# A graph layer on one core: shorter row scans, norms behind the first keys, queries mixed two chunks ahead

## The chip, the core and the metric

The kernel runs on one core of a Trainium2 chip. The core has a matrix engine (PE, with its weight loads PEld), a vector engine (DVE), an activation engine (ACT), a general engine (POOL[...]) and SyncE (SP), which here only issues DMAs. ACT and POOL issue DMAs too. The metric is the device time of one execution in microseconds, as the median of several.

## What is computed

One layer of a graph network with linear attention and a mixture of experts, all in float32, for 10,000 nodes with 512 features and 160,000 edges sorted by destination (more edges go to low node numbers: the destination is 10000 u², u uniform).

```
xn  = layernorm(x)
gnn = relu(segment_sum((xn @ W)[src] * edge_weight, dst) + bias)
q, k, v = split(xn @ w_qkv.T)            # 8 heads of 64
ctx = softmax(k over nodes).T @ v        # 64 x 64 per head
mix = layernorm((softmax(q) * 64**-0.5 @ ctx) @ w_out.T) * gamma
x1  = x + gnn + mix
out = x1 + sum_e weight_e * (gelu(layernorm(x1) @ W1_e + b1_e) @ W2_e + b2_e)
```

The six expert weights come from a router that sees the mean of the normalised rows of x1.

## The kernel before

**Chunks and tiles.** The nodes are cut into 20 chunks of 512 rows (the last has 272), a row of a chunk being partition p, sub-row s of 4. The edges are cut into 1250 tiles of 128. Edges are summed by windows: two tiles per window for the first 448 windows (`PAIRED`), one tile after that, so 802 windows; four windows make a group, 201 groups in all.

**Start.** Rows of x are loaded, normalised (DVE for the statistics, ACT and POOL for the rows) and stored to `xn_d` (`normal_rows`, L357). `norms` (L516) squares the 512 x 512 weights wk and then wq on ACT, sums the columns on PE and takes the maximum on DVE; `as_they_are` (L525) turns both into a factor 0 or 1, `usable`, spread to all partitions by a small product (L531). Every exponential of keys and queries is scaled by it (L765, L772). The two squares share one buffer, so the second can't be written before PE has read the first.

**Keys stage** (L744 to L793). For each chunk PE makes the keys (`pk`, 4 x 4 products of 128 x 512), the queries (`pq`, as many), the transposed rows of the next chunk, the context products `pc` (16), and the transposed queries, which ACT's queue stores to `qT_d`. From chunk 3 on, `place_edges` (L394) has prepared the edges: each edge's place in its window, `bases` (the first node of each window) and `jump` (the rows that a window skips). `count` collects checks whose total must be `ALL_GOOD`; otherwise a slow general path runs behind the branch at L615. `find_rows` (L444) finds for each node the row of its sum: for each of the 4 sub-rows one pass over all 802 windows compares `bases` with the node's number, multiplies by `jump` and sums up. It does five chunks as the edges are placed and then one per chunk.

**Edges.** For each tile POOL gathers 128 rows of `xn_d` (L485, 256 KB), DVE makes a selection matrix, and PE multiplies it with the rows (`pm`, L503). ACT copies a group's sums out and its queue stores them to `part_d`. There are 24 buffers for gathered rows. PE's order is the order of the program, written out by hand: after each product `work(us)` (L597) adds up the time of the products so far, and `edges_to` puts in as many groups as that time divided by `PACE` (0.93 us) allows. Nodes whose edges lie in several windows are put together by `carry` (L560), which reads stored sums back, adds and stores again.

**Mixing and node sums** (L872 to L965). `attention(c)` loads the transposed queries (`qT`, one buffer, SP's queue) and the rows of x (`xt`), multiplies the queries with the mixed context (`po`, 16 products), takes layer statistics and adds x; the result is `ot`. In its last quarter it calls `nodes_rows`, in which PE transposes the gathered node sums of the chunk in turn (`at` to `aT`) and POOL gathers the next chunk's by `row_of` (L865). Then `pg` multiplies `aT` with the graph weights (16 products), DVE adds bias, relu and `ot`, and SP stores x1 to `x1_d`. In this version attention runs one chunk ahead of the node sums: `po` 0, then for each c `po` c+1 and `pg` c. `far_enough` (L846) makes sure that the edges that a gather needs are summed; for chunk 18 all of them, with the last carry.

**Experts.** From L1233 on PE multiplies chunk after chunk, full to the end.

Of the kernel before, what the change touches and what calls it, by code (L numbers as in the profile page):

```python
# [9 lines left out]
F32 = mybir.dt.float32  # L10
I32 = mybir.dt.int32
AF = mybir.ActivationFunctionType
ALU = mybir.AluOpType
# [3 lines left out]

P = 128
SQ = 32
SUB = 4  # L20
EPS = 1e-5
HEAD = 64
QSCALE = HEAD ** -0.5
PAIRED = 448
GROUP = 4
WIN = P // GROUP
# [1 line left out]
EARLY = 3  # L28
ROWS_SOON = 5
PRODUCT = 0.83  # L30
PACE = 0.93

AT_HAND = [(5, 320), (7, 384), (9, 448), (11, 512), (13, 576), (14, 640), (15, 672), (16, 704), (17, 736), (18, 756)]
CARRIES = [0, 128, 224, 320, 384, 448, 512, 576, 640, 672, 704, 736, 756]
# [12 lines left out]
def gps_layer_kernel(  # L47
# [19 lines left out]
    nc = tc.nc  # L67
    N, D = x.shape
    NET = src.shape[1]
    KB = D // P  # L70
# [9 lines left out]
    chunks = []  # L80
# [6 lines left out]
    NCH = len(chunks)  # L87
# [64 lines left out]
    def behind(inst, other):  # L152

        tc.add_manual_dep(inst.ins, other.ins.name, mybir.DependencyInfo(
            mybir.DependencyClass.NoSync, mybir.DependencyReason.SCHED_ONLY), reason="order of work")
# [179 lines left out]
    with ExitStack() as ph:  # L335
# [50 lines left out]
        on_w = ep.tile([P, NET], F32, name="on_w")  # L386
        bases = ep.tile([P, NW + 1], F32, name="bases")
        jump = ep.tile([P, NW], F32, name="jump")
        count = ep.tile([P, 2 + len(AT_HAND)], F32, name="count")
        n_big = ep.tile([1, 2], F32, name="n_big")  # L390
        usable = ep.tile([P, 1], F32, name="usable")
        n_odd = ep.tile([1, 1], I32, name="n_odd")
# [1 line left out]
        def place_edges():  # L394
            nc.sync.dma_start(src_sb, src)
            nc.sync.dma_start(w_sb, edge_w)
            dst_sb = tmp.tile([P, NET], I32, name="dst_sb", tag="whole")
            nc.sync.dma_start(dst_sb, dst)
            row_sb = tmp.tile([P, NET], I32, name="row_sb")
            nc.sync.dma_start(row_sb, dst[0:1, :].to_broadcast([P, NET]))  # L400

            nc.vector.memset(bases[:, 0:1], 0.0)
            nc.vector.memset(bases[:, NW:], FAR)
            nc.vector.tensor_copy(bases[:, 1:PAIRED],
                                  row_sb[:, 2 : 2 * PAIRED].rearrange("p (w j) -> p w j", j=2)[:, :, 0])
            nc.vector.tensor_copy(bases[:, PAIRED:NW], row_sb[:, 2 * PAIRED :])
            gap = ew.tile([P, NW], F32, name="gap", tag="past", bufs=1)
            nc.vector.tensor_tensor(gap, bases[:, 1:], bases[:, :NW], ALU.subtract)
            nc.vector.tensor_copy(place, dst_sb)

            def by_window_of(t, per_window, o, op):

                nc.vector.tensor_tensor(
                    o[:, : 2 * PAIRED].rearrange("p (w j) -> p w j", j=2),
                    t[:, : 2 * PAIRED].rearrange("p (w j) -> p w j", j=2),
                    per_window[:, :PAIRED, None].to_broadcast([P, PAIRED, 2]), op)
                nc.vector.tensor_tensor(o[:, 2 * PAIRED :], t[:, 2 * PAIRED :], per_window[:, PAIRED:NW], op)

            by_window_of(place, bases, place, ALU.subtract)

            by_window_of(place, gap, on_w, ALU.is_equal)
            nc.vector.tensor_tensor(on_w, on_w, w_sb, ALU.mult)


            nc.vector.memset(jump[:, 0:1], 1.0)
            nc.vector.tensor_scalar(jump[:, 1:], gap[:, : NW - 1], -1.0, float(WIN), op0=ALU.mult, op1=ALU.add)


            good = tmp.tile([P, NET], F32, name="good", tag="whole")
            by_window_of(place, gap, good, ALU.is_le)  # L430
            nc.vector.scalar_tensor_tensor(good, place, 0.0, good, op0=ALU.is_ge, op1=ALU.mult)
            nc.vector.scalar_tensor_tensor(good, place, float(WIN - 1), good, op0=ALU.is_lt, op1=ALU.mult,
                                           accum_out=count[:, 0:1])
            nc.vector.tensor_scalar(good[:, :NW], gap, 0.0, None, op0=ALU.is_ge)
            nc.vector.scalar_tensor_tensor(good[:, : NW - 1], gap[:, : NW - 1], float(WIN), good[:, : NW - 1],
                                           op0=ALU.is_lt, op1=ALU.mult, accum_out=count[:, 1:2])

            for i, (n, w) in enumerate(AT_HAND):
                nc.vector.tensor_scalar(count[:, 2 + i : 3 + i], bases[:, w : w + 1],
                                        float(chunks[n][0] if n < NCH else N), None, op0=ALU.is_ge)  # L440

        ALL_GOOD = P * (NET + NW - 1 + len(AT_HAND))

        def find_rows(c, other):  # L444

            at = ew.tile([P, SUB], F32, name="at")
            for s in range(SUB):
                past = ew.tile([P, NW], F32, name="past", bufs=1)
                scan = nc.vector.scalar_tensor_tensor(
                    past, bases[:, :NW], node[:, c, s : s + 1], jump,  # L450
                    op0=ALU.is_le, op1=ALU.mult, accum_out=at[:, s : s + 1])
                if other:
                    behind(scan, other)
            nc.vector.tensor_tensor(at, at, node[:, c], ALU.add)
            nc.vector.tensor_scalar(row_of[:, c], at, float(ZERO_ROW), None, op0=ALU.min)

# [58 lines left out]

        def norms(i, w):  # L516

            sq = b_io.tile([P, KB, D], F32, name="sq", tag="ek")
            nc.scalar.activation(sq, w, AF.Square)
            pn = psum.tile([1, D], F32, name="pn", tag="ps")  # L520
            for kb in range(KB):
                nc.tensor.matmul(pn, ones, sq[:, kb, :], start=kb == 0, stop=kb == KB - 1)
            nc.vector.tensor_reduce(n_big[:, i : i + 1], pn, axis=AX.X, op=ALU.max)

        def as_they_are():  # L525


            nc.vector.tensor_scalar(n_big, n_big, NORM2, None, op0=ALU.is_le)
            nc.vector.tensor_tensor(n_big[:, 0:1], n_big[:, 0:1], n_big[:, 1:2], ALU.mult)
            pn = psum.tile([P, 1], F32, name="pn", tag="ps")  # L530
            nc.tensor.matmul(pn, until[0:1, :], n_big[:, 0:1], start=True, stop=True)  # L531
            nc.vector.tensor_copy(usable, pn)

# [202 lines left out]
            transposed(xnT, xn, chunks[c][1], psum, "ps")  # L736
            return xnT

        norms(0, wk)
        norms(1, wq)  # L740
        as_they_are()
        xn = rows_of(0)
        xnT = turned_rows(0, xn)
        for c, (_, r) in enumerate(chunks):  # L744
# [13 lines left out]
            if c + 1 < NCH:  # L758
                xn_next = rows_of(c + 1)
            ek = b_io.tile([P, SUB, D], F32, name="ek")  # L760
            for s in range(SUB):
                pk = psum.tile([P, D], F32, name="pk", tag="ps")
                times(pk, xnT, s, r, wk)
                work(KB * PRODUCT)
                nc.scalar.activation(ek[:r, s, :], pk[:r], AF.Exp, scale=usable[:r])  # L765
                nc.vector.tensor_tensor(kacc[:r], kacc[:r], ek[:r, s, :], ALU.add)
            qt = b_io.tile([P, SUB, D], F32, name="qt")
            for s in range(SUB):
                pq = psum.tile([P, D], F32, name="pq", tag="ps")
# [105 lines left out]
            return qT  # L875

        def rows_again(c):
            xt = io.tile([P, SUB, D], F32, name="xt")
            nc.sync.dma_start(xt[: chunks[c][1]], tokens(x, c))
            return xt  # L880

# [6 lines left out]
        def attention(c, beside):  # L888


            r = chunks[c][1]
            qT = queries_in(c)
            xt = rows_again(c)
            ot = io.tile([P, SUB, D], F32, name="ot", bufs=3)
            for s in range(SUB):
                if s == SUB - 1:
                    beside()
                po = psum.tile([P, D], F32, name="po", tag="ps")
                times(po, qT, s, r, mix)
                put_out(KB * PRODUCT)  # L900
                if c == s == 0:
                    held["at"] = gathered(0)
                nc.scalar.copy(ot[:r, s, :], po[:r, :])  # L903
            mv = small.tile([P, SUB, 2], F32, name="mv")
            row_stats(ot, r, mv)
            for s in range(SUB):
                nc.vector.scalar_tensor_tensor(ot[:r, s, :], ot[:r, s, :], mv[:r, s, 0:1],
                                               gamma_b[:r], op0=ALU.subtract, op1=ALU.mult)
                nc.vector.scalar_tensor_tensor(ot[:r, s, :], ot[:r, s, :], mv[:r, s, 1:2],
                                               xt[:r, s, :], op0=ALU.mult, op1=ALU.add)  # L910
            return ot

        ot_next = attention(0, lambda: None)
        for c, (_, r) in enumerate(chunks):
            ot, at = ot_next, held["at"]
            aT = io.tile([P, KB, SUB * P], F32, name="aT", bufs=1)

            def nodes_rows():
# [1 line left out]
                if c + 1 < NCH:  # L920
                    held["at"] = gathered(c + 1)

            if c + 1 < NCH:
                ot_next = attention(c + 1, nodes_rows)
            else:
                nodes_rows()

# [393 lines left out]
```

## Time and profile before

| What | Value |
|---|---|
| median of 3 runs | 3378.7 us (3378.27 to 3379.26) |
| profiled execution | 3381.44 us |
| its span in the trace | 3379.6 us |
| granted PE clock, mean | 0.988 of full |
| PE busy | 3270.7 us, 97% |
| DVE, ACT, POOL busy | 55%, 24%, 42% |
| keys begin on PE | 43.0 us |
| gathers of edges begin, end on POOL | 169.9, 1904.3 us |
| keys stage ends on PE | 1138.9 us |
| experts begin on PE | 2009.6 us |

In the lines that follow a timeline row gives start and duration in microseconds, engine, line, operation, output and input, the number of instructions, and in brackets the idle time of the engine just ahead and what ended it. A row of groups gives busy time and the mean of one in nanoseconds, then the idle time. A row of waits gives total, number and longest. In the slices each digit is the busy share of one fortieth of the span in tenths. Records of PE are half products: each float32 product has two.

### The profile page before, as it was taken

The page shows a single profiled execution, that of the slowest core. Times are in us where ns is not written, and L with a number is a line of the kernel's source. Part 1 is how long each engine was busy: PE and PEld are TensorE (multiplying, and loading weights), DVE is VectorE, ACT ScalarE, POOL GpSimd, SP SyncE. Part 2 cuts the span into 40 slices and gives each one's busy share as a digit, 9 for nine tenths or more (in the row PEclk, how much of TensorE's full clock was granted, in tenths as well). Part 3 has the DMA queues.
Part 4 walks back from the last instruction along what each step waited for, and adds up shares of the span by engine and source line. Part 5 has one row for each costly group of instructions (what it writes and reads, how often), then busy time and mean ns, then how long its engine had stood idle before and what let it go on. Part 6 is the DMA issues. An engine that isn't in the chain of part 4 may idle for free.

```text
span 3379.6 us, 37367 instructions
## 1 busy us (share of the span) xinstructions
PE 3270.7 (97%) x12969; PEld 1923.8 (57%) x12969; DVE 1842.5 (55%) x4771; ACT 797.3 (24%) x1626; POOL 1433.4 (42%) x1472
## 2 busy tenths in 40 slices
PE   6999999999999899999999999999999999999998
PEld 3444444444443333333333347888888888888886
DVE  7844545455545456666766576544554455445543
ACT  4412121212121121122222123222222222222211
POOL 6667777777777777777777420000000000000000
PEclk9999999999999999999999999999999999999999
DMA  9778888888878888999989751121212121212111
GB/s 363 262 231 254 275 258 279 257 272 263 268 241 262 290 291 304 309 329 325 329 313 329 235 163 50 50 63 50 88 50 63 54 84 50 63 60 78 50 39 40
DMA packets 218332, 644.96 MB, mean 191 GB/s; under 512 B 35486, under 2 KB 75422, under 8 KB 193786
## 3 DMA queue, kind: packets, MB, share of 16 engines
q0 software_dynamic: 108208, 354.02, 33.5%
q1 hardware_dynamic: 67656, 168.51, 15.2%
q10 hardware_dynamic: 42266, 119.91, 9.1%
q8 instruction: 106, 1.74, 0.2%
q14 instruction: 96, 0.79, 0.1%
HBM read 485.32 MB, written 157.00 MB: 190 GB/s over the span
## 4 chain that ended last, share of the span: by engine, by line
PE 54%; DMA 9%; issue 1%; DVE 1%; POOL 1%; ACT 0%; POOLq 0%; DVEq 0%; ACTq 0%; SPq 0%
PE px L1103 15%; PE pz L1103 10%; PE py L1103 10%; PE po L205 7%; DMA msg<-xn_d,src_sb 6%; PE pg L205 6%; PE pm L503 3%; PE ph L1103 2%; PE pt L197 1%; DMA z_d<-xt 1%; POOL msg L485 1%; DMA xt<-x_d 1%; DMA at<-part_d,row_of 1%; DMA x_d<-ot 0%; PE pcarry L568 0%
## 5 line engine op out<-in xcount | busy, mean ns | idle before, releaser
L485 POOL DMA_INDIRECT msg<-xn_d,src_sb x1250 | 1226.5, 981 | 424.8 <-issue 236.6
L503 PE MATMUL pm<-msg,sel 128*32 128x512 f32 x2504 | 356.2, 603 | 28.7 <-DMA msg<-xn_d,src_sb 28.6
L492 DVE TENSOR_SCALAR sel<-iota_w,place,w_sb 128x31 f32<-128x31 f32 x1250 | 305.9, 317 | 103.9 <-PE pm L503 103.7
L205 PE MATMUL po<-G,qT 128*128 128x512 f32 (+1 forms) x640 | 292.7, 604 | 8.0 <-DMA qT<-qT_d 8.0
L205 PE MATMUL pg<-wq,aT 128*128 128x512 f32 (+1 forms) x640 | 293.5, 607 | 5.9 <-ACT aT L199 5.9
L779 PE MATMUL pc<-xn,ek 128*128 128x512 f32 (+1 forms) x640 | 288.7, 601 | 3.7 <-DVE qt L190 3.7
L205 PE MATMUL pk<-wk,xnT 128*128 128x512 f32 (+1 forms) x640 | 285.7, 599 | 0.0
L205 PE MATMUL pq<-wq,xnT 128*128 128x512 f32 (+1 forms) x640 | 284.5, 597 | 0.0
L506 ACT COPY part<-pm 128x512 f32<-128x512 f32 x201 | 118.1, 587 | 629.7 <-PE pm L503 604.7
L503 PEld LDWEIGHTS pm<-msg,sel 128*32 128x32 f32 x2504 | 68.3, 109 | 282.2 <-issue 196.9
L205 PEld LDWEIGHTS pg<-wq,aT 128*128 128x128 f32 (+1 forms) x640 | 116.9, 189 | 182.9 <-issue 162.9
L205 PEld LDWEIGHTS po<-G,qT 128*128 128x128 f32 (+1 forms) x640 | 116.0, 189 | 171.0 <-issue 147.5
L205 PEld LDWEIGHTS pk<-wk,xnT 128*128 128x128 f32 (+1 forms) x640 | 118.1, 188 | 164.4 <-issue 153.1
L205 PEld LDWEIGHTS pq<-wq,xnT 128*128 128x128 f32 (+1 forms) x640 | 117.5, 187 | 165.3 <-issue 159.2
L1103 PE MATMUL px<-xnT,w_sb 128*128 128x256 f32 (+1 forms) x800 | 203.8, 377 | 6.4 <-DVE u L1138 6.3
L779 PEld LDWEIGHTS pc<-xn,ek 128*128 128x128 f32 (+1 forms) x640 | 118.7, 192 | 145.8 <-issue 141.7
L1103 PE MATMUL px<-w_sb,hh 128*128 128x256 f32 (+1 forms) x800 | 185.7, 379 | 0.0
L161 DVE BATCH_NORM_STATS2 st<-ot 128x6 f32<-128x512 f32 (+1 forms) x160 | 110.2, 689 | 138.4 <-ACT ot L903 137.5
L1103 PE MATMUL py<-xs,w_sum 128*128 128x256 f32 (+1 forms) x800 | 185.0, 374 | 0.0
L1103 PE MATMUL py<-w_sum,hh 128*128 128x256 f32 (+1 forms) x800 | 179.2, 379 | 0.0
L1103 PEld LDWEIGHTS px<-xnT,w_sb 128*128 128x128 f32 x800 | 150.3, 191 | 28.5 <-DVE u L1138 8.8
L1103 PEld LDWEIGHTS py<-w_sum,hh 128*128 128x128 f32 (+1 forms) x800 | 150.0, 188 | 22.7
(270 smaller groups left out, 4438.5 us busy)
## 6 DMA issues: line engine op xcount, KB each, us to landing
part_d<-part ACTq DMA_DIRECT2D x201, 256.0 KB
msg<-xn_d,src_sb POOLq DMA_INDIRECT x1250
xn<-in_x SPq DMA_DIRECT2D x19, 1024.0 KB
xn_d<-xn ACTq DMA_DIRECT2D x19, 1024.0 KB
qT_d<-qT ACTq DMA_DIRECT2D x19, 1024.0 KB
qT<-qT_d SPq DMA_DIRECT2D x19, 1024.0 KB
xt<-in_x SPq DMA_DIRECT2D x19, 1024.0 KB
x_d<-ot SPq DMA_DIRECT2D x19, 1024.0 KB
```

Source lines behind the costliest of these rows:

```text
L161: nc.vector.bn_stats(st[:r, s, :], t[:r, s, :])
L197: nc.tensor.transpose(pt[:, s * r : (s + 1) * r], t[:r, s, kb * P : (kb + 1) * P], ident[:r, :r])
L205: nc.tensor.matmul(po[:r, :], t[:, kb, s * r : (s + 1) * r], w[:, kb, :], start=kb == 0, stop=kb == KB - 1)
L485: nc.gpsimd.indirect_dma_start(out=m[k], out_offset=None, in_=xn_d, in_offset=bass.IndirectOffsetOnAxis(ap=src_sb[:, t0 + k : t0 + k + 1], ...
L492: nc.vector.tensor_scalar(sel[:, k, 1:], iota_w, place[:, t0 + k : t0 + k + 1], w_sb[:, t0 + k : t0 + k + 1], op0=ALU.is_equal, op1=ALU.mult)
L503: nc.tensor.matmul(pm[h * WIN : (h + 1) * WIN, :], sel[:, k, :], m[k] if k < len(m) else m[0], start=j == 0, stop=j == batch - 1, skip_gro ...
L506: nc.scalar.copy(part, pm)
L779: nc.tensor.matmul(pc, ek[:r, s, cb * P : (cb + 1) * P], xn[:r, s, :], start=s == 0, stop=s == SUB - 1)
L1103: nc.tensor.matmul(o, lhs[j], rhs[j], start=start and j == 0, stop=stop and j == n - 1, skip_group_check=True)
```

## The change

It has these parts:

- `find_rows` passes only over the windows that can hold the chunk's nodes: a range worked out from the expected distribution, ten tiles wider on both sides (`SPARE`), with one more instruction that adds what lies ahead of the range. Forty checks (`spans_hold`) join `count`. The scan's output no longer shares a buffer with `gap`.
- The norms of wk and wq, and the factor `usable`, are made after the four key products of chunk 0 instead of ahead of the transposes; the four exponentials and sums of chunk 0 follow them. The squares use the buffer `qT` instead of `ek`, and their sums the two banks of the edges.
- Attention runs two chunks ahead: `po` 0, `po` 1, then for each c `po` c+2 and `pg` c. `ot` has four buffers instead of three, `xt` one instead of two.
- `PACE` is 0.945 instead of 0.93.

```diff
-PACE = 0.93
+PACE = 0.945
...
         def find_rows(c, other):
             at = ew.tile([P, SUB], F32, name="at")
+            lo, hi = span(c)
             for s in range(SUB):
-                past = ew.tile([P, NW], F32, name="past", bufs=1)
+                past = ew.tile([P, WIDEST], F32, name="past_c", bufs=1)[:, : hi - lo - 1]
                 scan = nc.vector.scalar_tensor_tensor(
-                    past, bases[:, :NW], node[:, c, s : s + 1], jump,
+                    past, bases[:, lo + 1 : hi], node[:, c, s : s + 1], jump[:, lo + 1 : hi],
                     op0=ALU.is_le, op1=ALU.mult, accum_out=at[:, s : s + 1])
...
+            nc.vector.tensor_scalar(at, at, bases[:, lo : lo + 1], float(1 + lo * WIN), op0=ALU.subtract, op1=ALU.add)
...
+        def window_at(node, more):
+            tile_no = NET * (node / N) ** 0.5 + more
+            return min(max(int(tile_no / 2 if tile_no < 2 * PAIRED else tile_no - PAIRED), 0), NW)
+
+        def span(c):
+            return window_at(chunks[c][0], -SPARE), window_at(chunks[c][0] + SUB * chunks[c][1], SPARE)
+
+        def spans_hold():
+            for c, (b, r) in enumerate(chunks):
+                for i, w, op, edge in ((0, span(c)[0], ALU.is_le, b), (1, span(c)[1], ALU.is_ge, b + SUB * r)):
+                    at = 2 + len(AT_HAND) + 2 * c + i
+                    nc.vector.tensor_scalar(count[:, at : at + 1], bases[:, w : w + 1], float(edge), None, op0=op)
...
         def norms(i, w):
-            sq = b_io.tile([P, KB, D], F32, name="sq", tag="ek")
+            sq = b_io.tile([P, KB, D], F32, name="sq", tag="qT")
...
-            pn = psum.tile([1, D], F32, name="pn", tag="ps")
+            pn = psum_e.tile([1, D], F32, name="pn", tag="pm")
...
-        norms(0, wk)
-        norms(1, wq)
-        as_they_are()
...
+            sums = []
             for s in range(SUB):
                 pk = psum.tile([P, D], F32, name="pk", tag="ps")
                 times(pk, xnT, s, r, wk)
                 work(KB * PRODUCT)
-                nc.scalar.activation(ek[:r, s, :], pk[:r], AF.Exp, scale=usable[:r])
-                nc.vector.tensor_tensor(kacc[:r], kacc[:r], ek[:r, s, :], ALU.add)
+                sums.append(pk)
+                if c == 0 and s < SUB - 1:
+                    continue
+                if c == 0:
+                    norms(0, wk)
+                    norms(1, wq)
+                    as_they_are()
+                for i, pk in enumerate(sums):
+                    at = s + 1 - len(sums) + i
+                    nc.scalar.activation(ek[:r, at, :], pk[:r], AF.Exp, scale=usable[:r])
+                    nc.vector.tensor_tensor(kacc[:r], kacc[:r], ek[:r, at, :], ALU.add)
+                sums = []
...
-            xt = io.tile([P, SUB, D], F32, name="xt")
+            xt = io.tile([P, SUB, D], F32, name="xt", bufs=1)
...
-            ot = io.tile([P, SUB, D], F32, name="ot", bufs=3)
+            ot = io.tile([P, SUB, D], F32, name="ot", bufs=4)
...
-        ot_next = attention(0, lambda: None)
+        mixed = [attention(c, lambda: None) for c in range(2)]
         for c, (_, r) in enumerate(chunks):
-            ot, at = ot_next, held["at"]
+            ot, at = mixed.pop(0), held["at"]
...
-            if c + 1 < NCH:
-                ot_next = attention(c + 1, nodes_rows)
+            if c + 2 < NCH:
+                mixed.append(attention(c + 2, nodes_rows))
             else:
                 nodes_rows()
```

More of the change, by code (lines that the diff above doesn't have):

```diff
@@ L19 @@
 SQ = 32
+SPARE = 10
 SUB = 4
@@ L388, in gps_layer_kernel @@
         jump = ep.tile([P, NW], F32, name="jump")
-        count = ep.tile([P, 2 + len(AT_HAND)], F32, name="count")
+        count = ep.tile([P, 2 + len(AT_HAND) + 2 * NCH], F32, name="count")
         n_big = ep.tile([1, 2], F32, name="n_big")
@@ L406, in place_edges @@
             nc.vector.tensor_copy(bases[:, PAIRED:NW], row_sb[:, 2 * PAIRED :])
-            gap = ew.tile([P, NW], F32, name="gap", tag="past", bufs=1)
+            gap = ew.tile([P, NW], F32, name="gap", bufs=1)
             nc.vector.tensor_tensor(gap, bases[:, 1:], bases[:, :NW], ALU.subtract)
@@ L440, in place_edges @@
                                         float(chunks[n][0] if n < NCH else N), None, op0=ALU.is_ge)
-        ALL_GOOD = P * (NET + NW - 1 + len(AT_HAND))
+            spans_hold()
+        ALL_GOOD = P * (NET + NW - 1 + len(AT_HAND) + 2 * NCH)
+        WIDEST = 256
+        def window_at(node, more):
[8 more added lines that the diff above has]
+                    nc.vector.tensor_scalar(count[:, at : at + 1], bases[:, w : w + 1], float(edge), None, op0=op)
         def find_rows(c, other):
             at = ew.tile([P, SUB], F32, name="at")
+            lo, hi = span(c)
             for s in range(SUB):
-                past = ew.tile([P, NW], F32, name="past", bufs=1)
+                past = ew.tile([P, WIDEST], F32, name="past_c", bufs=1)[:, : hi - lo - 1]
                 scan = nc.vector.scalar_tensor_tensor(
-                    past, bases[:, :NW], node[:, c, s : s + 1], jump,
+                    past, bases[:, lo + 1 : hi], node[:, c, s : s + 1], jump[:, lo + 1 : hi],
                     op0=ALU.is_le, op1=ALU.mult, accum_out=at[:, s : s + 1])
@@ L529, in as_they_are @@
             nc.vector.tensor_tensor(n_big[:, 0:1], n_big[:, 0:1], n_big[:, 1:2], ALU.mult)
-            pn = psum.tile([P, 1], F32, name="pn", tag="ps")
+            pn = psum_e.tile([P, 1], F32, name="pn", tag="pm")
             nc.tensor.matmul(pn, until[0:1, :], n_big[:, 0:1], start=True, stop=True)
```

## The prediction

> **What bounds the kernel now.** I read the page's slices first, then the timelines of PE and POOL, then PE's waits. In the slices PE is full nearly everywhere, and POOL is steady until slice 23 and then silent:
>
> ```profile
> PE   6999999999999899999999999999999999999998
> POOL 6667777777777777777777420000000000000000
> ...
> L485 POOL DMA_INDIRECT msg<-xn_d,src_sb x1250 | 1226.5, 981 | 424.8 <-issue 236.6
> L503 PE MATMUL pm<-msg,sel 128*32 128x512 f32 x2504 | 356.2, 603 | 28.7 <-DMA msg<-xn_d,src_sb 28.6
> ```
>
> A gather takes POOL 0.98 us and 0.30 us to issue, so POOL's 0.75 share is a full engine. By its timeline the gathers run from 169.9 to 1904.3. In the keys stage (to 1138) PE is the slower: POOL's gaps over 0.7 us there end at "PE pm", 27 us in all. From 1138 on POOL hardly stops: 517 edge and 72 node gathers in 766.3 us, **1.30 us each**. There PE waits on landings. Its work in 1138.95 to 1917.3, warm and without waits, is some 688 us: 138 products of `po` and `pg` by 3.55 (490), edge sums 135, transposes 34, carries 18, context 12. That leaves 90 us of 778 for waits and cold clock. From 2009.6 PE is full to the end (the experts). So three stretches matter: the start, POOL's chain, and what PE has left after the last edge.
>
> ```profile
> 20.18 5.97 PE L522 MATMUL pn<-sq,ones 128*1 128x512 f32 x8 [20.18 <-ACT sq L519]
> 28.15 5.29 PE L522 MATMUL pn<-sq,ones 128*1 128x512 f32 x8 [2.00 <-ACT sq L519]
> 39.07 0.55 PE L531 MATMUL pn<-n_big,until 1*128 1x1 f32 x2 [5.63 <-DVE n_big L529]
> 39.55 3.68 PE L197 MATMUL pt<-ident,xn 128*128 128x128 f32 x16
> 43.02 15.12 PE L205 MATMUL pk<-wk,xnT 128*128 128x512 f32 x32
> ```
>
> This is PE's timeline at the start (start, duration): keys begin at 43.0, behind both norms, though wk was there at 18.1 (the Square that reads it) and chunk 0's rows were normalised at 15.9.
>
> ```profile
> PE pm L503 <- DMA msg<-xn_d,src_sb: 28.6, 21, 5.0
> ...
> PE po L205 <- DMA qT<-qT_d: 8.0, 1, 8.0
> PE pt L197 <- DVEq L615: 7.2, 1, 7.2
> ...
> PE pc L779 <- DVE qt L190: 3.7, 2, 3.2
> ```
>
> PE's waits (total, times, longest) are few; the longest in the middle are landings of messages, one load of qT, and the branch at L615.
>
> ```profile
> 413.75 1.05 DVE L449 SCALAR_TENSOR_TENSOR past<-bases,node,jump 128x802 f32<-128x802 f32 x1
> 413.88 1.74 POOL L485 DMA_INDIRECT msg<-xn_d,src_sb  x1 [0.30 <-DMA msg<-xn_d,src_sb]
> ...
> 1903.34 1.02 POOL L485 DMA_INDIRECT msg<-xn_d,src_sb  x1 [0.31 <-issue]
> 1944.66 0.95 POOL L865 DMA_INDIRECT at<-part_d,row_of  x1 [40.30 <-DMA b_sb<-in_b]
> ```
>
> ```profile
> 1915.45 1.93 PE L503 MATMUL pm<-msg,sel 128*32 128x512 f32 x6 [0.99 <-DMA msg<-xn_d,src_sb]
> 1917.31 8.15 PE L205 MATMUL pg<-wq,aT 128*128 128x512 f32 x16
> ...
> 2009.59 1.03 PE L1103 MATMUL px<-xs,w_sum 128*128 128x256 f32 x4
> ```
>
> Both engines at the end of the edges: the last gather is issued at 1904.3, its sum is done at 1917.3, and 92.3 us of PE's work still stand before the experts at 2009.6.
>
> **Norms behind the first keys.** Keys need the last odd row of chunk 0 (15.9) and then the 3.5 us that lay between the first transpose and `pk` before: 19.4. Keys 15.1 (as before, cold): 34.5. Norm of wk 3.5 (8 records by the warm 0.43): 38.0. The square of wq shares one buffer (now tag qT) with that of wk, so it can't start earlier: 1.9 of ACT plus a handover, PE idle 2.0: 40.0. Norm of wq 4.4: 44.4. Then DVE's chain to `n_big`, 1.0 of work, 5.6 before because other work was queued ahead; I take 3.3: 47.7. With the small product (0.55) and half a cold restart (0.9) the queries begin at 49.1 instead of 57.98: **-8.9**, between -4.7 (full 5.6, both restarts cold) and -13 (1.0, none). Queued behind the wait on PE are only the queries; behind it on ACT the four exponentials, which hold four of six banks, so two query products can go first.
>
> [...] after waits of 1.86 and 3.21 us the 16 records of `pc` at 123.85 took 8.80 instead of 7.03, and after 2.39, 0.48 and 0.48 us again 8.83. I take half of a 1.8 us loss, hence 4.4[...].
>
> **Short scans.** The 802-element scan holds DVE 0.98 us. Ranges worked out from L449's edges are 27 to 145 windows wide, mean 53; the nearest row, the same operation 128 wide (L565), takes 0.33, so 0.25 to 0.3 each, -0.72. Of DVE's packed stretch from 88 to 160, 20 scans save 14.4; 40 new checks cost 0.07 each (three of L439 take 0.26) = 2.8, the new subtraction 5 x 0.08: net -11.2. PE's waits there (1.86, 3.21, 2.39, 0.48, 0.48) and two cold restarts of 1.8 are 12 us, but PE also comes 8.9 earlier to a DVE that is only 8.4 earlier at the first `pc` and 11.3 at the second. So the edges stage begins **9 us** earlier (3 to 13), which is start and scans together. The last chunk's scans (3 us sooner at the branch) lie inside POOL's chain and give nothing; without that cover they'd give 3.
>
> [...] a gather beside a scan took 1.74 instead of 0.95, two per chunk, 15 chunks, 24 us of POOL. By the row I take POOL as full as its 24 buffers allow at the end of the keys[...].
>
> **PACE 0.945.** By the rules of L584 to L604 the keys end after 88 groups of 8 tiles instead of 90, and 6.7 tiles into the next (17 chunks x 48 products x 0.83, less 6 x 0.945, is 671.6; by 0.945, 710.7 tiles). PE saves 16 sums by 0.232 = 3.7. POOL, limited by buffers, is then 22 ahead: 726 gathers issued instead of 733, so 596 follow instead of 589: 7 x 1.30 = +9.1. Net **+5.4** on POOL's end, with the 9 earlier: 1900.7; last sum, by the same 13.0 of landing and work, 1913.7.
>
> **Queries two chunks ahead.** Ahead of the last edge now stand po 19's first quarter and all of pg 16: 7 products of 3.5 more. A second wait for qT (one buffer, 8.0, then `po` 6.33 instead of 3.60) appears as po 2 follows po 1 with no pg between; its DMA stands on SP as before. With 3.7 of sums PE has about 744 us of work against POOL's 788, so these are hidden in POOL's chain; without it they'd cost 10.7 plus nothing moved. xt's single buffer is asked for one chunk period (some 40 us) after its last reader, against a load of 8: nothing. POOL's gathers of node rows keep their places among the edges (at 17 behind tile 1248). SP's store of x1 and the load of qT are no further apart than now.
>
> After the last sum PE has: two products po 19 (7.0), transposes 1.9, wait for the last carry, carry 2.0, po 3.5, pg 17 13.8, transposes 1.8, pg 18 13.8, statistics and transposes 2.0, the wait for ACT 5.9 as now, pg 19 16.0. The carry needs the last part written and read: 1917.3 to 1923.5 for the write, some 4 for the reads, so 10.5 against PE's 8.8: wait 1.7. Sum 69.3 instead of 92.3: **-23.0**. Gather 18 lands about 14.6 after the carry and PE wants it after 17.3; gather 19 stands behind the weights' issues, as before, and lands under ACT's 5.9. If that cover is gone, 3 to 6 us. DVE has some 49 us of work in these 69.
>
> **Sum.** -9.0 + 5.4 - 23.0 = -26.6. Bounds of what I can't see (DVE crowded in the shorter tail, POOL stopping on full buffers when PE's two qT waits fall together) are 0 to +10; I take 5: -21.6 on the span of 3379.6, 3358.0. The profiled execution took 3381.4, 1.8 around the span, and stands 2.7 over the median 3378.7; from the median, **3357 us**, 3350 to 3365 alone.
>
> **Rivals.** (1) The start is swallowed and the tail half used: rows and DVE keep chunk 3 where it was (-3), DVE sets the tail (-12), PACE +5.4: -9.6, 3369. For it: DVE is 46 of 50 us busy in 50 to 100. (2) Everything: 13 at the start, no tail loss, -30.6, 3348. (3) Nothing: POOL's chain ends later by what the tail gives, 3379; needs POOL 20 us late, against its full rate. (4) Slower: PE becomes the bound in the mixing stage, if qT of each chunk comes late behind other waits on SP. Price: 18 chunks by the 8 us of a bare qT load, less the 44 us that PE has to spare, 100; it decides from 2.4 us per chunk on. Against it: qT is issued 19.5 us ahead of use now (1226.6 for 1246.1) and lands in 8. Taken at 2.9 us per chunk it gives 3388.
>
> **How the numbers follow.** A change of 0.2% (6.8 us) is about what a measurement tells from none. Forecast 0.55, (1) 0.20, of which a third ends within 0.2%, (2) 0.15, (3) 0.04, (4) 0.06: faster 0.83, same 0.11, slower 0.06. Leaving out 2 in 10 (some of (2)'s best end, part of (1) and (3), and (4)) gives 3344 to 3371.
>
> **What would show it.** Keys at 19 to 21 us; queries near 49; edge sums from about 198; the last gather near 1900; a second wait of `po` on qT near 1200; after the last sum about 70 us to the experts. It is wrong if the last gather comes after 1910, if PE waits on DVE in the tail, or if `pm` no longer waits for messages at all.

## The result, and the profile after

| | before | after |
|---|---|---|
| median | 3378.98 us (4 runs, 3378.27 to 3384.84) | 3362.78 us (4 runs, 3361.17 to 3366.16) |
| ratio after / before | | 0.995, 95% interval 0.9932 to 0.9967 |
| profiled execution | 3381.44 us | 3361.17 us |
| its span | 3379.6 us | 3359.4 us |
| chunk 3's keys begin | 193.15 | 182.82 |
| keys stage ends | 1138.9 | 1124.7 |
| last gather of edges ends | 1904.3 | 1903.5 |
| last edge sum ends on PE | 1917.3 | 1914.9 |
| experts begin on PE | 2009.6 | 1984.7 |
| experts, begin to end of span | 1370.0 | 1374.7 |

The kernel is 16.2 us faster by the medians and 20.2 by the two profiled spans. The runs fell into two conditions of the chip, a first one in which the kernel before takes 3375 to 3379 us, and a second one in which it takes 3648 to 3651 us and PE, DVE and ACT pause while edges are gathered (151 us on PE in the changed kernel); the table above, the kernel before profiled again and the run with half of the gathers are of the first, the other experiments of the second, and times are compared within a condition only.

First the slices and groups of the kernel after.

```profile
PE   7999999999999879999999989999999999999998
...
POOL 6677777777777677777777520000000000000000
...
L505 POOL DMA_INDIRECT msg<-xn_d,src_sb x1250 | 1214.0, 971 | 434.5 <-issue 238.8 <-PE pm L523 70.4 <-DMA msg<-xn_d,src_sb 59.2
L523 PE MATMUL pm<-msg,sel 128*32 128x512 f32 x2504 | 345.8, 602 | 12.2 <-DMA msg<-xn_d,src_sb 11.9
```

The shape is as before: PE full, POOL steady and then silent. PE waits 11.9 us for messages where it waited 28.6, and POOL waits 70.4 us for PE to free buffers where it waited 54.0.

PE's timeline at the start shows keys at 18.62 and queries at 51.09, behind a wait of 7.78 us.

```profile
18.62 15.07 PE L206 MATMUL pk<-wk,xnT 128*128 128x512 f32 x32
33.62 3.59 PE L542 MATMUL pn<-sq,ones 128*1 128x512 f32 x8
39.21 3.59 PE L542 MATMUL pn<-sq,ones 128*1 128x512 f32 x8 [2.00 <-ACT sq L539]
50.58 0.58 PE L551 MATMUL pn<-n_big,until 1*128 1x1 f32 x2 [7.78 <-DVE n_big L549]
51.09 15.97 PE L206 MATMUL pq<-wq,xnT 128*128 128x512 f32 x32
```

PE's waits (total, times, longest) show the second load of `qT`, and one that no line of before had in this size, `px` for DVE's `u`.

```profile
PE po L206 <- DMA qT<-qT_d: 16.9, 2, 8.6
...
PE pm L523 <- DMA msg<-xn_d,src_sb: 11.9, 16, 2.5
PE px L1131 <- DVE u L1166: 10.9, 4, 6.7
PE pn L551 <- DVE n_big L549: 7.8, 1, 7.8
PE pt L198 <- DVEq L635: 6.7, 1, 6.7
```

PE's timeline from the last edge sum into the experts:

```profile
1913.31 1.67 PE L523 MATMUL pm<-msg,sel 128*32 128x512 f32 x8 [0.21 <-DMA msg<-xn_d,src_sb]
1914.90 7.08 PE L206 MATMUL po<-G,qT 128*68 128x512 f32 x16
...
1965.78 0.98 PE L198 MATMUL pt<-ident,at 68*128 68x68 f32 x3 [4.35 <-DMA at<-part_d,row_of]
...
1984.67 1.03 PE L1131 MATMUL px<-xs,w_sum 128*128 128x256 f32 x4
...
1996.75 2.07 PE L1131 MATMUL px<-xnT,w_sb 128*128 128x256 f32 x4 [6.73 <-DVE u L1166]
```

The tail from the last sum to the experts is 69.8 us instead of 92.3. Twelve microseconds into the experts PE stands for 6.73 us. ACT's timeline says why: its copy to `u` waits for the store of the last chunk's x1, because `u` now lies in memory that held that chunk's `ot`.

```profile
1995.87 0.37 ACT L1165 COPY u<-px 128x256 f32<-128x256 f32 x1 [8.13 <-DMA x_d<-ot]
```

In the kernel before ACT waited 7.49 us for the same store, but at the first gelu, where PE needed nothing of it.

### The profile page after: what moved, and what is told of

Read it like the earlier page. It is cut to its first block, busy times and chain, and to the rows that moved or that the text cites. A ratio compares the mean times of both kernels' runs of the same rounds, so it can differ in the third digit from the quotient of the medians.

```text
span 3359.4 us, 37435 instructions
## 1 busy us (share of the span) xinstructions
PE 3257.2 (97%) x12969; PEld 1927.2 (57%) x12969; DVE 1792.6 (53%) x4831; ACT 797.0 (24%) x1626; POOL 1414.0 (42%) x1472
## 3 DMA queue, kind: packets, MB, share of 16 engines
q8 instruction: 106, 1.74, 0.2%
## 5 line engine op out<-in xcount | busy, mean ns | idle before, releaser
L505 POOL DMA_INDIRECT msg<-xn_d,src_sb x1250 | 1214.0, 971 | 434.5 <-issue 238.8
L523 PE MATMUL pm<-msg,sel 128*32 128x512 f32 x2504 | 345.8, 602 | 12.2 <-DMA msg<-xn_d,src_sb 11.9
```

Of the source, the lines that this page charges most:

```text
L505: nc.gpsimd.indirect_dma_start(out=m[k], out_offset=None, in_=xn_d, in_offset=bass.IndirectOffsetOnAxis(ap=src_sb[:, t0 + k : t0 + k + 1], ...
L523: nc.tensor.matmul(pm[h * WIN : (h + 1) * WIN, :], sel[:, k, :], m[k] if k < len(m) else m[0], start=j == 0, stop=j == batch - 1, skip_gro ...
```

## The experiments

### One part undone: norms, scans

```diff
+        norms(0, wk)
+        norms(1, wq)
+        as_they_are()
...
-                if c == 0:
-                    norms(0, wk)
-                    norms(1, wq)
-                    as_they_are()
```

> The changed kernel with the norms back ahead of chunk 0's transposes and keys. Theory (the start is passed on through PE to the edges stage): queries begin some 7 us later, at 58 instead of 51.1; DVE's lead takes back a little, so chunk 3's keys come 5 to 7 us later than 182.8, the keys end at 1130 instead of 1124.7, and the span is 3364 to 3366 instead of 3359.4. Rival (the start is swallowed by POOL's chain of gathers or by DVE's work from 88 to 160): chunk 3's keys or the last gather stay within 1.5 us, and the span is 3359 to 3361.

```diff
-                    past, bases[:, lo + 1 : hi], node[:, c, s : s + 1], jump[:, lo + 1 : hi],
+                    past, bases[:, :NW], node[:, c, s : s + 1], jump,
```

> The changed kernel with the scans over all 802 windows again, and no range checks. By the row of the kernel before (a gather beside a long scan takes 1.74 us instead of 0.95): the long gathers come back, two per chunk over 15 chunks; DVE's stretch from 88 to 160 is 11 us longer and chunk 3's keys come about 5 us later; the last gather is 3 to 9 us later and the span 3364 to 3368. [...] only the start counts, about 3 us, span 3362.

Both ran in the second condition: ratios to the kernel before 1.0006 (0.9989 to 1.0024) and 1.0042 (1.0023 to 1.006), where the changed kernel had 0.9994 (0.9971 to 1.0018). The start lies almost wholly ahead of the first gather (172.6 us) and is the same in both conditions (chunk 3's keys of the changed kernel at 182.82 in the first, 183.22 in the second). Chunk 3's keys begin at 188.12 with the norms in front and at 190.41 with the long scans. So the norms' place is worth some 5 us at chunk 3 and the scans some 7, against 10.3 for both in the first pair of profiles. These are single profiles: over all that have both changes, chunk 3's keys begin anywhere from 182.4 to 186.3. For the norms, what comes of it at the end can't be told from 1.0006 against 0.9994.

For the scans it can: 1.0042 lies above the interval of the changed kernel, some 17 us more by the ratios (each to the kernel before beside it), and the loss goes beyond the start. What the rest of it consists of in this condition is not shown, since POOL is not the bound there (see below). One cost of the long scans is seen in DVE's and POOL's timelines of the kernel that has them:

```profile
384.34 1.05 DVE L465 SCALAR_TENSOR_TENSOR past<-bases,node,jump 128x802 f32<-128x802 f32 x1
...
385.44 1.05 DVE L465 SCALAR_TENSOR_TENSOR past<-bases,node,jump 128x802 f32<-128x802 f32 x1
...
387.62 1.05 DVE L465 SCALAR_TENSOR_TENSOR past<-bases,node,jump 128x802 f32<-128x802 f32 x1
```

```profile
384.68 1.53 POOL L502 DMA_INDIRECT msg<-xn_d,src_sb  x1 [1.22 <-PE pc L804]
386.51 0.95 POOL L502 DMA_INDIRECT msg<-xn_d,src_sb  x1 [0.30 <-issue]
387.77 1.73 POOL L502 DMA_INDIRECT msg<-xn_d,src_sb  x1 [0.30 <-issue]
```

The first and the third gather start 0.34 and 0.15 us into a scan, last 1.53 and 1.73 us, and both end 0.8 us after the scan does. The one between them starts as the second scan ends and takes 0.95. Not every gather beside a scan is slowed: in the kernel before the 20 longer ones started 0.13 to 0.61 us into a scan, and of the 29 others, among them gathers that were under way when a scan began, 28 kept 0.94 to 0.97 us. Of 51 gathers that overlap a long scan here, 17 are longer, by 12 us in all (before: 20 of 49, by 14 us), where the prediction had 30 and 24 us. Over all edges POOL's gathers take 1225.2 us with long scans and 1210.6 with short ones (second condition), and 1226.5 and 1214.0 in the first: 12 to 15 us.

The scans are not alone in this. In the changed kernel 80 gathers are still longer than 1.1 us, by 28 us in all, and 79 of them start during another DVE instruction that reads two tiles of SBUF, such as the sum of `kacc` and `ek` (27 of the 45 gathers that start during it). The rows speak against the last figure of the expectation, 3362 for a loss at the start alone.

### PACE alone undone

```diff
-PACE = 0.945
+PACE = 0.93
```

> The changed kernel with PACE at 0.93 again. Theory: the keys end after two more groups of edge sums, POOL's last gather comes about 5 us earlier, but at this pace the last groups fall so that seven more products (24.5 us) stand behind the last edge sum: the tail from the last sum to the experts is about 94 us instead of 69.8, and the span 3375 to 3379: most of the gain of the queries two chunks ahead is gone. Rival (the pace counts for a few us of POOL alone): the tail stays near 70 us and the span is 3354 to 3359.

The tail is 94.2 us, as the order by the program's rules said it must be: seven products stand behind the last sum again. But the time is no different (1.0004, 0.9984 to 1.0023), since in this condition the stretch from the keys' end to the last sum takes 894.6 us instead of 930.7: 36 us less for 28 us less of PE's work in it. POOL's part of the theory was wrong here: counted from the keys' end, the last gather comes not 5 us earlier but 37. That fits PE, not POOL, as the bound of that stretch in this condition, so that what is moved out of the tail is paid in front of the last sum. The 36 us are of single profiles, and the kernel of the next section, profiled twice, differs from itself by 22 us in this stretch.

### One chunk ahead again

```diff
-        mixed = [attention(c, lambda: None) for c in range(2)]
+        mixed = [attention(c, lambda: None) for c in range(1)]
...
-            ot = io.tile([P, SUB, D], F32, name="ot", bufs=4)
+            ot = io.tile([P, SUB, D], F32, name="ot", bufs=3)
```

> The changed kernel with attention one chunk ahead again (two xt buffers, three ot buffers), PACE left at 0.945. Theory: the last sum stays within 3 us of 1914.9; the last groups are then forced in ahead of the gathers that need them, so the carry of the last chunk waits some 10 us and the tail is about 83 us instead of 69.8; the 4.7 us at the experts' start, where DVE waits on ACT and ACT on a store out of ot, go away: span 3366 to 3373. Rival (the second product in advance gives nothing, POOL and the experts' start set the end): span 3355 to 3361.

> u_ahead once more, as a neighbour of the run above (one chunk ahead, PACE 0.945). Theory on a chip like the first: PE's work before the last sum falls by about 16 us but POOL's chain keeps the last sum where it is, 788 to 792 us from the keys' end; the tail is 86 us as before instead of 70; u's wait of 6.7 us stays or goes with the buffers (5 either way): span 3370 to 3376. Rival (PE is the bound): the last sum comes 16 us earlier and the span is within 5 us of 3359.

Both ran in the second condition: 1.0032 (1.0011 to 1.0052) and 1.0047 (1.0028 to 1.0066), slower than the kernel before. The tails are 85.4 and 84.6 us (83 expected), with a wait of 8.18 us for the last carry in the first. Here the last groups are forced in front of the gather that needs them, and the last sum is not the earlier for the work that left: 930.2 and 952.1 us from the keys' end, against 930.7. PE's pauses differ from profile to profile (123 and 106 us in this stretch, against 94 in the changed kernel), so these three don't settle what the moved work costs. The wait for `u` is gone as the first text said, and the experts take 1367.9 and 1368.1 us to the end of the span. So PACE 0.945 with one chunk ahead, and the better start on top, is slower than the kernel before, which has PACE 0.93. The second text's figures for the first condition weren't tested.

### Is it bytes? Half of each row

```diff
-                        m[k] = pools["m"].tile([P, D], F32, name="msg")
+                        m[k] = pools["m"].tile([P, D // 2], F32, name="msg")
...
-                            out=m[k], out_offset=None, in_=xn_d,
+                            out=m[k], out_offset=None, in_=xn_d.rearrange("n (h d) -> (n h) d", h=2),
```

> Each gather fetches only half a row (1 KB instead of 2 KB from each of 128 rows), and PE multiplies that half twice with the selection, so the sums over edges are not those of the layer; the number of gathers, of sums and their order stay. Theory (POOL's time[...] sets the pace from the keys' end to the last gather): the last gather ends within 5 us of that of the changed kernel beside it, and the span within 5 us. Rival (the DMA engines or the memory's bandwidth set it): the 163 MB saved bring the last gather forward by 50 us or more on a chip like the first, and by most of the 290 us on one like that of the last group.

Each half is multiplied twice, so that PE does the same multiplications in twice as many records for the edge sums (2504 more), and is busy 3406.6 us instead of 3359.1. From the keys' end to the last gather it takes 921 us against 912 for the changed kernel in the same condition, and the whole is 1.0124 (1.0097 to 1.0152). With 163 MB less nothing came earlier: in this condition the bytes don't set the pace. The span grew by 38 us where the theory said 5 at most, which fits PE's 47 us more with PE as the bound. How far POOL's chain reaches could not be seen here, but the price of a gather on POOL could. First the changed kernel in this condition, then the one with half rows:

```profile
L505 POOL DMA_INDIRECT msg<-xn_d,src_sb x1250 | 1210.6, 968 | 680.1 <-issue 294.3
```

```profile
L505 POOL DMA_INDIRECT msg<-xn_d,src_sb x1250 | 1211.8, 969 | 727.0 <-issue 284.1
```

A gather holds POOL for as long with 1 KB per row as with 2 KB.

### Half of the gathers

```diff
+                        if k % 2:
+                            m[k] = m[k - 1]
+                            continue
                         m[k] = pools["m"].tile([P, D], F32, name="msg")
```

> The changed kernel without every second gather of edge rows; the neighbour's rows are multiplied in their place, so 625 gathers fewer and other sums, while PE, DVE and ACT do the same work. On a chip like the last one: if the stalls of PE, DVE and ACT for which the profile shows no cause come from the gathers' traffic, PE's fall from some 150 us to under 75, and the span by 100 us or more; if they are the chip's own, they stay, and the span falls by less than 40. On a chip like the first: if POOL's chain is the bound from the keys' end on but PE is close behind it, the last sum comes 12 to 40 us earlier (PE's waits for messages, 11.9, and part of its waits for qT), and no more.

This one ran in the first condition, and it is the run that decides there: 3318.71 us, 0.9829 (0.9813 to 0.9846). Keys end at 1125.2, the last sum at 1869.9 instead of 1914.9. With POOL out of the way PE needs **744.7 us** from the keys' end to the last sum; the changed kernel takes 790. So the gathers set the last sum there, with PE 45 us behind them. That it is POOL's own time and not their landing is read from POOL's timeline in the changed kernel: beyond the 0.30 us ahead of each gather POOL stands for only 9.7 us of the 778.8 from the keys' end to the last gather, 7.5 of them at the branch, although the DMA engines are busy for 0.92 of the time from 1140 to 1900. The expectation of 12 to 40 us was too low, and its reason shows how a page can mislead. These are the groups of gathers and edge sums of this run:

```profile
L508 POOL DMA_INDIRECT msg<-xn_d,src_sb x625 | 606.0, 970 | 921.6 <-PE pm L526 747.5 <-issue 112.4 <-PE pt L198 28.8
L526 PE MATMUL pm<-msg,sel 128*32 128x512 f32 x2504 | 311.1, 602 | 0.1
```

The same 2504 products are "busy" 345.8 us in the changed kernel and 311.1 here. In the stretch behind the keys alone, 1096 records of `pm` take 176.4 us there and 141.9 here, though one record lasts as long in both (602 ns over the whole run): they overlap less. The 34.6 us between are waits for messages that the view of PE counts as work; the view of the weight loads has them:

```profile
PEld pm L523 <- DMA msg<-xn_d,src_sb: 50.7, 68, 3.4
```

This is the changed kernel; with half of the gathers the same line has 0.8 us.

### The kernel before, once more

> The kernel before, profiled in the neighbourhood of the last runs. Theory for a chip like theirs (PE with stalls of its own, not POOL's chain of gathers, sets the time from the keys' end to the last sum): that stretch takes some 28 us less than the 931 us of the changed kernel, about 903 (seven products less, 24.5, and two groups of sums less, 3.7), and the tail 92 instead of 70, so that moving the queries ahead gives nothing there. Rival (POOL's chain sets it, as on the first chip): the stretch takes about as long as in the changed kernel, 925 to 935, less the 7 gathers.

It was meant for the second condition and fell into the first, so the theory for the second is not tested by it. It shows the spread of single profiles instead: span 3370.5 against 3379.6 of the same kernel, of which 8.0 lie between the keys' end and the last sum (770.4 against 778.4), while the experts take 1370.0 us in both. PE's wait for `u` at the second `px` is 1.04 us.

### The changed kernel in the second condition, and `u` elsewhere

> The changed kernel itself, as the neighbour of the next three. If the chip is as in the first profiles (granted clock 0.988, a gather every 1.25 to 1.30 us without gaps after the keys), 3360 us and 0.995 of the kernel before. If it is as in the runs with one part undone (clock 0.955, the kernel before at 3651 us, both PE and POOL idle among the edges), the parts that lie outside the edges keep their worth: some 7 us at the start and 22 to 25 us in the tail, so 3620 to 3630 and a ratio of 0.992 to 0.995.

The expectation of 0.992 to 0.995 was wrong: 0.9994 (0.9971 to 1.0018). Start and tail kept their worth (chunk 3's keys at 183.22, tail 70.0), so it is lost in between. PE's timeline there has pauses inside one product, whose operands all lie in SBUF:

```profile
1499.72 0.59 PE L206 MATMUL po<-G,qT 128*128 128x512 f32 x1
1500.85 1.02 PE L206 MATMUL po<-G,qT 128*128 128x512 f32 x2 [0.53 <-issue]
1502.28 2.56 PE L206 MATMUL po<-G,qT 128*128 128x512 f32 x5 [0.41 <-issue]
```

`issue` stands where nothing that the profile shows ended the wait, which the text below calls a wait without a releaser. Such waits add up to 151 us on PE, and to none in the profiles of the first condition. POOL now waits for PE's sums, and PE's weight loads hardly wait for messages:

```profile
POOL msg L505 <- PE pm L523: 200.2, 91, 17.7
...
PEld pm L523 <- DMA msg<-xn_d,src_sb: 13.3, 14, 2.0
```

against 70.4 and 50.7 in the first condition. So PE, with its pauses, is the bound here. Seven products moved ahead of the last sum would then cost there what they save behind it, which fits a ratio of 0.9994 with a tail of 70.0.

```diff
+            h21 = sp.tile([P, HALF], F32, name="h21")[:, :h]
+            if c == p == 0:
+                sp.tile([P, 112], F32, name="gap", bufs=1)
             u = sp.tile([P, HALF], F32, name="u")[:, :h]
```

> The changed kernel with the experts' tiles h21 and a gap of 448 bytes placed ahead of u, so that u no longer lies where chunk 19's rows (ot) are being stored. Theory: ACT's copy to u does not wait for that store (8.13 us before), DVE's u is ready some 8 us earlier, PE's wait of 6.7 us at the second group of px goes, and the experts end 4.7 us earlier: 3355 against 3359.4 (or 0.1% below the changed kernel beside it). ACT's wait for the store moves to the first gelu into h21 and is hidden. Rival (another wait of the same length stands behind it, as DVE's statistics or the table load): no change, within 1 us.

Beside it: 0.9972 (0.9953 to 0.9991), and PE's wait is gone. First the changed kernel, then the one with `u` elsewhere:

```profile
2281.02 2.07 PE L1131 MATMUL px<-xnT,w_sb 128*128 128x256 f32 x4 [6.76 <-DVE u L1166]
```

```profile
2279.11 1.13 PE L1131 MATMUL px<-xnT,w_sb 128*128 128x256 f32 x4 [1.04 <-DVE u L1169]
```

ACT's wait for the store moved to the gelu into `h21`, as said, and is hidden:

```profile
2283.94 0.51 ACT L1152 ACTIVATE h<-v,b_sb 128x256 f32<-128x256 f32 x1 [3.04 <-DMA x_d<-ot]
```

From the experts' first product to the end it is 1370.5 us instead of 1376.0. The cause of PE's wait is shown by the waits; that the whole kernel gets faster is likely, though not shown, since the two intervals overlap. With the next kernel it is the one whose interval lies below the kernel before in this condition; neither was run in the first.

```diff
-            at = io.tile([P, SUB, D], F32, name="at")
+            at = io.tile([P, SUB, D], F32, name="ot", bufs=4) if c == NCH - 1 else io.tile([P, SUB, D], F32, name="at")
...
+                if c == NCH - 3:
+                    held["last"] = gathered(NCH - 1)
+                    experts_weights()
```

> As u_place, and the gather of chunk 19's node sums is issued ahead of the experts' weights, into a free ot buffer. Theory: PE's wait of 4.35 us for that gather goes too, the weights come 5 us later and are hidden: 4.5 us less than u_place, 3350 on a chip like the first (0.992 of the kernel before). Rival (PE then waits for ACT's 5.9 us that stood behind it before, or for the weights' sums at the experts' start): 0 to 1 us less than u_place.

0.9981 (0.9964 to 0.9999), no better. The rival held: PE no longer waits for the gather, and waits for ACT instead.

```profile
2244.07 1.20 PE L198 MATMUL pt<-ident,ot 68*128 68x68 f32 x16
2251.15 16.64 PE L206 MATMUL pg<-wq,aT 128*68 128x512 f32 x32 [5.88 <-ACT aT L200]
```

### One group of sums ahead of the branch

```diff
         edges_to(past(CARRIES[FIXED] // GROUP, LAG) + 1)
+        edges_to(done[0] + 1)
         keys_ctx.close()
...
             transposed(GT, G, P, psum, "ps")
-            edges_to(done[0] + 1)
```

> The changed kernel with u moved as in u_place, and the first group of edge sums of the mixing stage put ahead of the branch instead of behind the transposes that follow it. Theory (on a chip like the first, POOL's gathers set the last sum, and the 7.8 us in which POOL stood at full buffers while PE stood at the branch are part of that chain): POOL's stop at the branch falls under 1 us, the last gather and the last sum come 6 to 8 us earlier, and with the 4.7 of u the span is 3346 to 3350, 0.9905 to 0.992 of the kernel before. Rival (POOL makes up for the stop later, or PE is the bound by then): the last sum stays within 2 us of the changed kernel's 790 us from the keys' end, and only u's 4.7 us come: 3354 to 3356.

In the second condition, where POOL is not the bound: 0.9988 (0.997 to 1.0007), last sum 933.5 us from the keys' end as without the move. PE's wait at the branch was 18.27 us in this profile, ACT's copy of the moved group came 11 us after PE had ended it, and POOL stood for 12.16 us. Nothing was gained. Whether the 7.8 us at the branch can be had in the first condition stays open.

## Why the prediction came out as it did

Predicted 3357 us, measured 3362.78; the span was to fall by 21.6 us and fell by 20.2, the median by 16.2. Only 1.4 of the 5.8 us between are what the sum missed of the spans. Some 4 are the base: the profile of before that the sum was made against lies 2.5 above its median (its repetition is 9 us shorter), and the profile of after 1.6 below its own. So the close agreement of the spans is in part luck, and the parts below, each read from one profile, are good to a few us only.

- **Bound.** Right in the first condition: POOL's 526 edge and 72 node gathers behind the keys take 778.8 us, 1.30 each, and PE needs 744.7 by the run with half of the gathers, where the text had 744. Of these the text writes out 716 (688, 24.5 and 3.7) and does not itemise the other 28, so an agreement within 1 us is partly luck. That PE's slack was there to take is why the queries ahead cost nothing.
- **Start, -9.0.** Chunk 3's keys came 10.3 us earlier. Its parts were off against each other. Queries began at 51.1, not 49.1, though keys began at 18.6, not 19.4: the chain to `n_big` kept PE 7.8 us, where 3.3 was taken, because DVE's reduction of wq's sums came only at 48.28, behind other work in its order, and the queries then took 15.97 us, the first 4.0 of them at a granted clock of 0.50. The norm of wq took 3.59 where 4.4 was taken, but not in every run (see the last section). The runs with one part undone give norms some 5 us and scans some 7 at chunk 3.
- **Scans beside gathers.** The row held, as shown above; the size was half of what the text worked out (12 to 15 us of POOL for 24), because only 20 of the 49 gathers that overlap a scan in the kernel before were longer, the ones that started 0.13 to 0.61 us into it, and two per chunk was too many.
- **PACE, +5.4.** 724 gathers were issued at the keys' end (726 said) and the last gather ended 2.8 us later than said, less than the 8.0 us by which the two profiles of before differ in this stretch. A stop of POOL stands in between that the sum put only into its allowance: 7.8 us at full buffers while PE stood at the branch.
- **Tail, -23.0.** 69.8 us for 69.3, 22.5 us less than before. Every item was there, but for the wait on the gather of chunk 19 (4.35 us), said to land under the wait for ACT: it took the place of that wait, as the later run with the gather moved forward shows by giving ACT's wait back.
- **Allowance, 5 of 0 to 10.** Right in size by luck, since the cause was another. DVE was not crowded: PE waits for none of its results between the last sum and the experts. The experts took 4.7 us longer to the end of the span because of where a tile lies: with four `ot` buffers and one `xt`, the memory of `u` fell to the last chunk's `ot`, and ACT waits for its store. The step that failed is the one that weighed the buffers of `ot` and `xt` by when they are free for chunks, and not by what is laid over them afterwards. Every kernel profiled that keeps two chunks ahead and leaves `u` there has 1374.7 to 1378.9 us behind the experts' begin, and the others 1367.0 to 1370.6; among these the three two-chunk kernels with `h21` put there instead.
- **Rivals.** (1), (2) and (3) lie outside what was measured: the start was not swallowed, and the tail was used whole. (4), PE as the bound in the mixing stage, was excluded in the first condition by 45 us. In the second it is what happens, not through `qT` as the text had it but through pauses, and there the change brings nothing (0.9994). Its 3388 does not follow from its own working: 18 chunks by 2.9 are 8 us more than PE's spare 44, and these go on the forecast (3365), not on the time before, as long as the tail still gives its part.

## What to carry to other kernels

Work that is moved in front of a point is free only while another engine's chain ends at that point: find the slack by taking half of that chain away (here 45 us), since PE's busy time, 97% of the span, held 34.6 us of waits that only the weight loads' waits showed. When the number of buffers in a pool changes, look at what later tiles are laid over which of them, and which transfer still reads it. A gain that rests on such a slack goes when the condition of the chip changes the bound (here a ratio of 0.995 in the first and of 0.9994 in the second). A wait of the engine that is full to the end costs its time in either condition: the one for `u` made the experts 4.7 us longer in the first and 5.5 in the second.

## What the runs showed of the hardware that was not expected

- In the second condition PE, DVE and ACT pause without a releaser, 151 us on PE, 199 on DVE and 122 on ACT in the changed kernel, and PE only while edges are gathered: none before 175 us and none after the last edge sum, behind which the experts' products ran at a granted clock of 0.99 with as little idle (19 us of 1365) as in the first (26 of 1374). PE's fall inside products with all operands in SBUF (0.41 and 0.53 us within one `po` above), and halving the gathered bytes left them (137 us). The transfers of the kind `instruction` on queue q8 are as many in both conditions (106, 1.74 MB in the changed kernel). The run with half of the gathers, which might have told whether the gathers are needed for the pauses, fell into the first condition. Where the record names the chip, the second condition was met on two and the first on a third, so that it may belong to the chip. What the cause is stays open.
- After the same idle of 2.00 us the eight records of wq's norm took 3.59 us in eleven profiles and 5.29 in three (both of the kernel before and the one with `PACE` at 0.93). In the first profile of the kernel before (5.29) the granted clock was 0.50 from 28.40 us on, 0.25 us into the norm, for 3.41 us; in that of the changed kernel (3.59) it was 1.00 through the idle and the norm, until 44.85. In these two traces every stretch at half clock lasted 3.41, 6.83 or 10.24 us, but for the one that the end of the trace cuts off. Why the same idle of 2.00 us was followed by the longer time in three profiles and not in the others is not shown; that it was free in the changed kernel was luck.
